# Projections to dt two at a time on two row quarters of the matmul array, with a re-laid opening and order, in a one-core decoder layer

## The chip, the cores and the metric

The kernel runs on one core of one Trainium2 chip. Times are microseconds on the device. The time before is the median of three runs: 1557.06 us (1556.51 to 1564.02). TensorE is called PE below, VectorE DVE, ScalarE ACT, GpSimd POOL, and the engine that only issues transfers SP.

## The reference, cut to what matters

A decoder layer of three post-norm blocks over 4 sequences of 512 tokens of width 512, all in float32: causal differential attention (8 head pairs of 128, four groups of keys and values), a Mamba-like selective scan over a second input `ctx`, and a mixture of 16 experts with a shared expert. The change sits in the second block:

```python
x = einsum('bld,ed->bel', ctx, in_proj_w)               # 256 -> 512 channels
x = silu(conv4_causal(x) + conv_b)
x_dbl = einsum('bdl,ed->bel', x, x_proj_w)              # 512 -> 16 + 16 + 16 rows
dt_low, Bm, Cm = split(x_dbl, [16, 32], axis=1)
dt = softplus(einsum('brl,dr->bdl', dt_low, dt_proj_w) + dt_proj_b)   # 16 -> 512 channels
state = state * exp(dt * A) + (dt * x) * Bm             # 512 steps, 16 states a channel
y = (sum(state * Cm) + D * x) * silu(z)
```

The contraction of the projection to dt is over 16 rows only.

## The kernel before, in words

The kernel does not call the engines directly. The class `Notes` records every instruction as a step with a key (about when it is wanted, plus a correction by result and engine from the table `SHIFT`), and the method `order` plays all steps against a list of costs and takes, for each engine, the ready step with the lowest key whose buffers are free. The result is a fixed order on each engine; on the chip each engine runs its own list strictly in order and waits for semaphores. So each engine's list depends on the keys, on `SHIFT` and on the buffers in each pool. Line 358 of the profile (`trace`) issues all of them, so lines in the profile are told apart by tile names, not by line numbers.

A float32 matmul in the source becomes two passes over the array, each with its own weight load; the profile counts passes. A projection to a 128 x 512 result over 512 rows is 4 matmuls, thus 8 passes.

The work falls in two stretches. For about two thirds of the time 16 units of attention (4 groups x 4 sequences) run on PE: projections `ps_qk` (q and k) and `ps_v`, scores `s`, transposes `pt`, values `po`, transposes `pt_o`, output projection `ps_out`. Beside them runs `scan(b)` for each sequence: `ps_in` (in-projection), copies to `xm`, four taps on ACT and DVE into `y`, silu (`sgc`), `ps_x` (48 rows), the copy `xd`, four matmuls `ps_dt` on 16 rows, softplus on ACT and DVE, and 32 scan steps on DVE. Then `experts(b)` runs: `pt_y`, `pt_x`, `ps_gate`, and for every expert `pg`, `ph`, `pa`; at the end `ps_y` and the last layer norm.

PSUM: `ps_in`, `ps_qk`, `ps_v`, `ps_x`, `ps_dt`, `ps_out` and others share the tag `mm` with three buffers, each free again when ACT or DVE has read it.

What stands around the opening: SP issues the first transfers in the listed order; PE starts with `ps_in` and goes on with `ps_qk`, `ps_x`, `ps_qk`, `ps_v`. DVE runs the taps, the silu products `y`, some small preparations (`lp`, `ls`, `nlam`, `a_neg`, which belong to the lambda of the attention and to A), and then adds the bias into `v`, which frees the PSUM of `ps_v`. POOL adds the output bias into the four residuals (`res<-res,obb`, 128 x 2048 each).

Of the kernel before, what the change touches and what calls it, by code (L numbers as in the profile page):

```python
# [20 lines left out]
ENGINES = ("tensor", "vector", "scalar", "gpsimd", "sync")  # L21

SHIFT = {
    "aT.s": 15.4, "a_neg.s": 12.1, "a_neg.v": -7.8, "bc.s": 7.4, "bq.s": -3.3, "bvb.s": -2.6, "cT.s": -3.5,
    "cf.v": -1.7, "cw.s": -2.2, "da.g": -4.8, "da.s": -1, "db.s": 4.2, "dsk.s": 2.1, "dt.s": -2.1, "dt.v": -7.7,
    "du.v": 21.2, "e.s": 7.6, "e.v": -2.1, "gb.s": -1.2, "h.v": -4.3, "ht.v": -6.5, "kT.s": 3.9, "l.v": 2.1,
    "ln_mv.v": -14.5, "ln_nb.v": -33.8, "ln_rs.g": -2.5, "ln_st.v": 4.7, "ln_ve.v": -21.4, "lo.v": 12.6, "lp.v":
    2.2, "ls.s": -1.8, "ls.v": -6.6, "lt.s": 3, "m.v": -3.7, "ms.v": -4.3, "nlam.v": -8.1, "o.s": -12.8, "oT.s":
    0.7, "obb.s": 17, "ow.s": -1.2, "pT.s": -2.7, "pa.t": 1, "pg.t": -2.1, "pg_s.t": -8.4, "ph.t": 2.8, "ph_s.t":
    3.2, "po.t": -7.2, "pr.s": -9.5, "pr.v": -13, "ps_dt.t": -0.1, "ps_gate.t": -18.9, "ps_in.t": -1.8,  # L30
    "ps_out.t": 5.1, "ps_qk.t": 1.3, "ps_v.t": 2.1, "ps_x.t": 12.8, "ps_y.t": 2.9, "pt.t": -0.3, "pt_o.t": 2.7,
    "pt_w.t": -7.1, "pt_x.t": 1.5, "pt_y.t": -5.9, "qT.s": 0.6, "relu.s": 20.5, "relu_s.s": -3.8, "res.g": -0.4,
    "res.s": -5.4, "res.v": -1.8, "rp.v": -16.4, "rs.g": 6.5, "rs.v": -12.2, "s.t": 0.9, "sc.v": 4, "sg.s": -1.5,
    "sg.v": 4.3, "sgc.s": 3.9, "sh.v": 7.5, "sp.v": 15.5, "sq.s": -16.2, "sub.s": -33.5, "sub.v": -9.9, "v.v":
    1.5, "w.s": 6.4, "wT.s": -1.1, "w_dg.s": 0.9, "w_dt.s": 6.5, "w_e.s": 23.5, "w_in.s": -30.8, "w_s.s": -0.3,
    "w_u.s": -4.7, "w_xp.s": 1.8, "wb.s": 10.2, "wq.s": 2.4, "wv.s": 5.9, "x2T.s": -13.1, "xd.s": 17.9, "xl.s":
    2.9, "xm.g": 1.7, "xm.s": 7.8, "xr.s": -1, "xw.v": 3.9, "y.g": -4.6, "y.s": 7.9, "y.v": -9.9, "yb.s": 5.6,
    "yb.v": 2.7,
}
B, S, HID = 4, 512, 512  # L40
NT = S // P
# [124 lines left out]
def cost(engine, name, out, ins, kw):  # L166

    n = columns(out) if isinstance(out, View) else 0
    psum = any(isinstance(v, View) and v.buf.pool.psum for v in ins)
    if engine == "tensor":  # L170
        if name == "transpose":
            return 0.11 * max(1, n / 128), 0.35, 0.0
        return max(n * 0.00168, 0.13), 0.35, 0.0
    if name == "dma_start":
        size = max(v.shape[0] * columns(v) * 4 if isinstance(v, View) else 0 for v in (out, *ins))
        add = kw.get("accum_op") is not None
        return {"sync": 0.45, "gpsimd": 0.95, "scalar": 0.1}[engine], 4.2 if add else 2.3, size / 230e3 * (1 + add)
    if engine == "gpsimd":
        if any(v is ALU.pow for v in ins):
            return 1.3, 0.5, 0.0  # L180
        return 0.15 + 0.0026 * n, 0.5, 0.0
    if engine == "scalar":
        wide = isinstance(kw.get("scale"), View) or isinstance(kw.get("bias"), View)
        return (
            0.19 + 0.00079 * n + (0.1 if wide else 0.0) + (0.15 if kw.get("accum_out") is not None else 0.0), 0.3, 0.0
        )
    if name == "tensor_tensor_scan":
        return 0.05 + 0.00223 * n, 0.25, 0.0
    if name in ("tensor_reduce", "bn_stats"):
        n = columns(ins[0])  # L190
    if n <= 8:
        return 0.2, 0.25, 0.0
    if name == "scalar_tensor_tensor":
        return 0.12 + 0.00125 * n, 0.25, 0.0
    if name == "tensor_scalar" and not psum:
        return 0.1 + (0.00085 if any(isinstance(v, View) for v in ins[1:]) else 0.00058) * n, 0.25, 0.0
    return 0.13 + (0.00108 if psum else 0.0011) * n + (0.1 if name == "tensor_tensor_reduce" else 0.0), 0.25, 0.0


class Notes:  # L200
# [7 lines left out]
    def note(self, engine, name, args, kw):  # L208
        s = Step()
        s.engine, s.name, s.args, s.kw, s.at = engine, name, args, kw, len(self.steps)  # L210
        out = kw["out"] if "out" in kw else args[0]
        rest = [a for a in args if a is not out] + [v for k, v in kw.items() if k not in ("out", "accum_out")]
        outs = [v for v in (out, kw.get("accum_out")) if isinstance(v, View)]
        ins = [v for v in rest if isinstance(v, View)]
# [38 lines left out]
    def order(self, keys, window=100.0):  # L253
# [24 lines left out]
        while events:  # L278
# [11 lines left out]
            for e in ENGINES:  # L290
# [4 lines left out]
                for s in ready[e]:  # L295
# [10 lines left out]

                    if all(
                        b in live
                        or free[b.pool, b.tag]
                        and (b.pool.psum or b in due[b.pool, b.counts[-1]][: free[b.pool, b.counts[-1]]])  # L310
                        for b in s.bufs
                    ):
                        best, least = s, rank
# [39 lines left out]
    def trace(self):  # L353
        done = self.order([s.key for s in self.steps])[0]
        assert len(done) == len(self.steps), "the order does not come to an end"
        for s in done:
            get = lambda v: v.get() if isinstance(v, View) else v
            getattr(getattr(self.nc, s.engine), s.name)(  # L358
                *[get(a) for a in s.args], **{k: get(v) for k, v in s.kw.items()}
            )  # L360
# [11 lines left out]
def decoder_kernel(  # L372
# [79 lines left out]
    def load_cT(b):  # L452
        return load([P, 2, S], ctxT[b].rearrange("(c p) t -> p c t", p=P), "h", "cT", 5)

    nc.key = -40.0
    bq = load([P, 32], bqkv, "bq")
    cw = load([P, ND, KC], convw, "cw")
    cb = load([P, ND], convb, "cb")
    w_in, cT0 = [], sb.tile([P, 2, S], "h", "cT", 5)
    for c in range(2):  # L460
        w_in.append(load([P, DI], inT[c * P : (c + 1) * P, :], "c2", "w_in", C2))
        nc.sync.dma_start(out=cT0[:, c, :], in_=ctxT[0, c * P : (c + 1) * P, :])
    xT0 = sb.tile([P, 4, S], "t8", "xT")
    wk0 = load_k(0)
    for c in range(4):
        nc.sync.dma_start(out=xT0[:, c, :], in_=xT[0, c * P : (c + 1) * P, :])
    wq0 = load_q(0)
    wv0 = load_v(0)
    w_xp = load([P, ND, 48], xpT.rearrange("(c p) n -> p c n", p=P), "w_xp")
    lt = load([P, 2, 2, HD], lam4.partition_broadcast(P).rearrange("p (a c d) -> p a c d", a=2, c=2), "qT", "lt", 2)  # L470
    sub = load([P, 2], subln, "sub")
    w_dt = load([DTR, DI], dtT, "c2", "w_dt", C2)
    db = load([P, ND], dtb, "db")
    dsk = load([P, ND], dskip, "dsk")
    a_neg = load([P, ND, NST], alog, "a_neg")
# [30 lines left out]
    def layernorm(src, dst, tiles=range(NT)):  # L506
# [12 lines left out]
        for i in tiles:  # L519
            nc.scalar.activation(  # L520
                dst[:, i, :], src[:, i, :], AF.Identity, bias=nb[:, i : i + 1], scale=rs[:, i : i + 1]
            )


    qk_scale = HD ** -0.5
# [121 lines left out]
    def scan(b):  # L647
# [23 lines left out]
            nc.vector.tensor_tensor(y[k], y[k], sg, ALU.mult)  # L671
        for d in range(ND):
            nc.tensor.matmul(
                px[:48, :], lhsT=w_xp[:, d, :], rhs=y[d // 2][:, d % 2, :], start=(d == 0), stop=(d == ND - 1)
            )
        xd = sb.tile([48, S], "c2", "xd", C2)
        nc.scalar.copy(xd, px[:48, :])
        nc.sync.dma_start(out=bc_d[b].rows(), in_=xd[DTR:48, :])


        nc.key = t_scan(b) - SOFTPLUS
# [1 line left out]
        for k in range(2):  # L683
            dt = sb.tile([P, 2, S], f"dt{k}", "dt")
            du = sb.tile([P, 2, S], f"du{k}", "du")
            lo = sb.tile([P, 2, S], "h", "lo", 5)
            for j in range(2):
                d = 2 * k + j
                pd = ps.tile([P, S], "mm", "ps_dt", 3)
                nc.tensor.matmul(pd, lhsT=w_dt[:, d * P : (d + 1) * P], rhs=xd[:DTR, :], start=True, stop=True)  # L690
                nc.scalar.activation(du[:, j, :], pd, AF.Abs, bias=db[:, d : d + 1])
                nc.scalar.activation(dt[:, j, :], pd, AF.Relu, bias=db[:, d : d + 1])
            nc.scalar.activation(du, du, AF.Exp, scale=-1.0)
# [51 lines left out]
    def experts(b):  # L745
# [26 lines left out]


        nc.key += 10.0
        pls, xr = [], sb.tile([P, NT, LAT], "pT", "xr", 2)
        for k in range(2):
            pl = ps.tile([P, 2, 256], "mm", "ps_gate", 3)
            for i in range(2):
# [165 lines left out]
```

## Time and profile before

| What | Before |
|---|---|
| Median of three runs | 1557.06 us (1556.51 to 1564.02) |
| The profiled execution: its own time, and its span from the first to the last instruction | 1558.77 us, 1557.0 us |
| PE busy with passes | 1534.4 us, 99% of the span, 4928 passes |
| DVE, ACT, POOL busy | 1204.0, 953.2, 193.9 us (77%, 61%, 12%) |
| Granted PE clock, mean | 0.992 |
| DMA moved | 196.18 MB, mean 126 GB/s |
| `ps_dt`: passes, busy | 32, 18.8 us |
| `ps_x`: passes, busy | 32, 16.9 us |

A busy row for PE counts each pass from its start to its modelled end. The ends overlap the next pass, so what a pass costs in a full stream is the distance between two starts, which is shorter than its listed duration. The clock column of a stretch is 1.00 when PE had its full clock and 0.50 when the throttle gave half.

### The profile page before, as it was taken

How to read it: one execution, taken by the hardware profiler on the slowest of the kernel's cores; microseconds unless marked ns; L12 is line 12 of the kernel's file. 1: busy time of each engine (PE TensorE's matmuls, PEld its weight loads, DVE VectorE, ACT ScalarE, POOL GpSimd, SP SyncE). 2: the span in 40 equal slices, each digit the busy share in tenths (PEclk: the TensorE clock that was granted, in tenths of full speed). 3: DMA queues.
4: the chain of work that ended last, by engine and by line, in shares of the span. 5: the costliest groups of instructions: out<-in, count | busy, mean ns of one | idle time of the engine just before them, and what ended most of it. 6: DMA issues, size and time to landing. Idle time of an engine off the chain costs nothing.

```text
span 1557.0 us, 15843 instructions
## 1 busy us (share of the span) xinstructions
PE 1534.4 (99%) x4928; PEld 846.0 (54%) x4928; DVE 1204.0 (77%) x2036; ACT 953.2 (61%) x2096; POOL 193.9 (12%) x208
## 2 busy tenths in 40 slices
PE   7999999999999999999999999999999999999998
PEld 2665665655656566565655555555545445445443
DVE  6559998777999887888988989999999962534433
ACT  3586566566756656576656658676967553444343
POOL 4011121101111111111111021211111100000000
PEclk9999999999999999999999999999999999999999
DMA  7126676525467763646765555665776851541341
GB/s 266 55 68 117 123 157 143 127 59 119 81 135 158 150 123 88 128 87 127 178 144 114 107 116 119 128 165 112 179 170 138 196 168 55 159 129 61 117 126 49
DMA packets 105523, 196.18 MB, mean 126 GB/s; under 512 B 10896, under 2 KB 45712, under 8 KB 105440
## 3 DMA queue, kind: packets, MB, share of 16 engines
q1 hardware_dynamic: 87008, 128.06, 29.1%
q0 software_dynamic: 18432, 67.12, 25.0%
q8 instruction: 39, 0.64, 0.2%
q14 instruction: 44, 0.36, 0.1%
HBM read 119.25 MB, written 75.89 MB: 125 GB/s over the span
## 4 chain that ended last, share of the span: by engine, by line
PE 96%; DVE 3%; ACT 0%; DMA 0%; issue 0%; SPq 0%; POOLq 0%; ACTq 0%
PE ps_qk L358 21%; PE ps_out L358 14%; PE s L358 9%; PE po L358 9%; PE ps_v L358 7%; PE pa L358 7%; PE ph L358 7%; PE pg L358 7%; PE ps_y L358 3%; PE pt L358 2%; PE pg_s L358 2%; PE ph_s L358 2%; PE pt_o L358 2%; PE ps_in L358 2%; PE ps_dt L358 1%; PE ps_gate L358 1%
## 5 line engine op out<-in xcount | busy, mean ns | idle before, releaser
L358 DVE TENSOR_TENSOR_SCAN h<-da,h 128x1024 f32<-128x1024 f32 x128 | 292.7, 2286 | 2.9 <-ACT da L358 0.4
L358 PE MATMUL ps_qk<-xT,wq 128*128 128x512 f32 x512 | 242.2, 594 | 0.0
L358 PE MATMUL ps_out<-ow,oT 128*128 128x512 f32 x512 | 238.1, 596 | 0.0
L358 POOL DMA_DIRECT2D y<-h x128 | 111.6, 872 | 795.1 <-DVE h L358 568.5
L358 ACT ACTIVATE da<-dt,a_neg 128x512 f32<-128x512 f32 (+1 forms) x256 | 175.1, 716 | 29.9 <-DVE h L358 25.9
L358 DVE TENSOR_TENSOR ht<-relu,ph 128x512 f32<-128x512 f32 x128 | 87.6, 685 | 125.3 <-PE ph L358 91.8
L358 ACT ACTIVATE relu<-pg 128x512 f32<-128x512 f32 x128 | 76.0, 593 | 160.4 <-PE pg L358 160.0
L358 PE MATMUL s<-kT,qT 128*128 128x384 f32 (+3 forms) x512 | 169.8, 440 | 1.1 <-DVE nm L358 1.1
L358 DVE CUSTOM_DVE_ANT_0 e<-s,mask 128x128 f32<-128x128 f32 (+3 forms) x256 | 118.9, 485 | 54.7 <-PE s L358 50.9
L358 PE MATMUL po<-v,pT 128*128 128x256 f32 x640 | 160.3, 381 | 0.4 <-ACT pT L358 0.4
L358 ACT ACTIVATE e<-e,nm 128x128 f32<-128x128 f32 (+3 forms) x256 | 142.0, 557 | 28.2 <-DVE nm L358 27.1
L358 DVE TENSOR_TENSOR h<-h,bc 128x1024 f32<-128x1024 f32 x128 | 156.2, 1220 | 1.3
L358 DVE TENSOR_TENSOR h<-du,bc 128x1024 f32<-128x1024 f32 x128 | 155.9, 1218 | 0.1
L358 PEld LDWEIGHTS po<-v,pT 128*128 128x128 f32 x640 | 121.7, 191 | 61.9 <-issue 35.2
L358 PEld LDWEIGHTS ps_out<-ow,oT 128*128 128x128 f32 x512 | 93.9, 192 | 83.7 <-issue 78.9
L358 PEld LDWEIGHTS ps_qk<-xT,wq 128*128 128x128 f32 x512 | 92.3, 191 | 77.3 <-issue 70.1
L358 PE MATMUL pa<-ht,w_e 128*128 128x512 f32 x256 | 130.8, 593 | 0.1
L358 PE MATMUL ph<-xw,w_e 128*128 128x512 f32 x256 | 130.3, 592 | 0.0
L358 PE MATMUL pg<-xl,w_e 128*128 128x512 f32 x256 | 129.4, 592 | 0.0
L358 PEld LDWEIGHTS s<-kT,qT 128*128 128x128 f32 x512 | 88.8, 192 | 63.5 <-issue 48.7
L358 PE MATMUL ps_qk<-xT,wk 128*128 128x512 f32 x256 | 120.9, 592 | 0.0
L358 ACT ACTIVATE sq<-po 128x256 f32<-128x256 f32 x128 | 48.7, 381 | 115.4 <-PE po L358 114.6
(121 smaller groups left out, 2084.0 us busy)
## 6 DMA issues: line engine op xcount, KB each, us to landing
y<-h POOLq DMA_DIRECT2D x128, 512.0 KB, 7.9
bc<-bc SPq DMA_DIRECT2D x64, 512.0 KB, 6.3
wb<-w SPq DMA_DIRECT2D x64, 256.0 KB, 3.4
xT<-in_xT_dram SPq DMA_DIRECT2D x15, 1024.0 KB, 7.8
w_e<-in_rwgT_dram SPq DMA_DIRECT2D x64, 128.0 KB, 2.2
w_e<-in_rw1T_dram SPq DMA_DIRECT2D x64, 128.0 KB, 2.3
w_e<-in_rw2T_dram SPq DMA_DIRECT2D x64, 128.0 KB, 2.5
wq<-in_wqkvT_dram SPq DMA_DIRECT2D x8, 512.0 KB, 5.9
```

Source lines behind the costliest of these rows:

```text
L358: getattr(getattr(self.nc, s.engine), s.name)(*[get(a) for a in s.args], **{k: get(v) for k, v in s.kw.items()})
```

## The change

1. The weights of the projection to x (`w_xp`) grow from 48 to 96 columns: the 16 dt columns and 16 that follow them go to columns 0 to 31, the same again to 32 to 63, and B and C to 64 to 95, so that `xd` holds the dt rows twice, at partitions 0 and 32. The weights `w_dt` are loaded twice, to partitions 0 and 32.
2. Two matmuls of `ps_dt` are noted as one step `pair`: it takes two `mm` buffers at once and issues the two matmuls one right behind the other, the first on rows 0 to 15, the second on rows 32 to 47.
3. The opening: eight matmuls of the identity on itself (`warm`) stand first on PE; the transfers of the first `ctx` halves (`cT`) are issued by ACT instead of SP; `bq` is loaded later, `w_in` first.
4. The tile `xr` of the experts moves from the pool tag `pT` to `c2`.
5. `SHIFT` has new values throughout, so the order on all engines is a new one.

```diff
-    "aT.s": 15.4, "a_neg.s": 12.1, "a_neg.v": -7.8, "bc.s": 7.4, "bq.s": -3.3, "bvb.s": -2.6, "cT.s": -3.5,
...
+    "aT.s": -4.1, "a_neg.s": 14.4, "a_neg.v": -15.4, "bc.s": 5.7, "bq.s": -18.3, "bvb.s": 8.1, "cT.s": -3.2,
...
     if engine == "tensor":
+        if name == "pair":
+            return 0.15 + n * 0.00168, 0.35, 0.0
...
-                        or free[b.pool, b.tag]
+                        or free[b.pool, b.tag] >= (2 if s.name == "pair" and b.pool.psum else 1)
...
+            if s.name == "pair":
+                for k in range(0, len(s.args), 3):
+                    out, lhsT, rhs = (get(v) for v in s.args[k : k + 3])
+                    self.nc.tensor.matmul(out, lhsT=lhsT, rhs=rhs, start=True, stop=True)
+                continue
...
-    nc.key = -40.0
-    bq = load([P, 32], bqkv, "bq")
-    cw = load([P, ND, KC], convw, "cw")
-    cb = load([P, ND], convb, "cb")
+    nc.key = -60.0
     w_in, cT0 = [], sb.tile([P, 2, S], "h", "cT", 5)
     for c in range(2):
         w_in.append(load([P, DI], inT[c * P : (c + 1) * P, :], "c2", "w_in", C2))
-        nc.sync.dma_start(out=cT0[:, c, :], in_=ctxT[0, c * P : (c + 1) * P, :])
+        nc.scalar.dma_start(out=cT0[:, c, :], in_=ctxT[0, c * P : (c + 1) * P, :])
+    nc.key = -50.0
+    cw = load([P, ND, KC], convw, "cw")
+    cb = load([P, ND], convb, "cb")
+    nc.key = -40.0
...
+    bq = load([P, 32], bqkv, "bq")
...
-    w_xp = load([P, ND, 48], xpT.rearrange("(c p) n -> p c n", p=P), "w_xp")
+    w_xp = sb.tile([P, ND, 96], "w_xp")
+    for to, src in ((0, 0), (32, 0), (64, DTR)):
+        nc.sync.dma_start(
+            out=w_xp[:, :, to : to + 32], in_=xpT[:, src : src + 32].rearrange("(c p) n -> p c n", p=P)
+        )
...
-    w_dt = load([DTR, DI], dtT, "c2", "w_dt", C2)
+    w_dt = sb.tile([48, DI], "c2", "w_dt", C2)
+    for row in (0, 32):
+        nc.sync.dma_start(out=w_dt[row : row + DTR, :], in_=dtT)
...
+    nc.key = -60.0
+    pw = ps.tile([P, S], "tr", "warm", 1)
+    for i in range(8):
+        nc.tensor.matmul(pw[:, :P], lhsT=ident, rhs=ident, start=True, stop=True)
...
-                px[:48, :], lhsT=w_xp[:, d, :], rhs=y[d // 2][:, d % 2, :], start=(d == 0), stop=(d == ND - 1)
+                px[:96, :], lhsT=w_xp[:, d, :], rhs=y[d // 2][:, d % 2, :], start=(d == 0), stop=(d == ND - 1)
...
-        xd = sb.tile([48, S], "c2", "xd", C2)
-        nc.scalar.copy(xd, px[:48, :])
-        nc.sync.dma_start(out=bc_d[b].rows(), in_=xd[DTR:48, :])
+        xd = sb.tile([96, S], "c2", "xd", C2)
+        nc.scalar.copy(xd, px[:96, :])
+        nc.sync.dma_start(out=bc_d[b].rows(), in_=xd[64:, :])
...
-            for j in range(2):
+            pds, both = [ps.tile([P, S], "mm", "ps_dt", 3) for _ in range(2)], []
+            for j, pd in enumerate(pds):
+                d, row = 2 * k + j, slice(32 * j, 32 * j + DTR)
+                both += [pd, w_dt[row, d * P : (d + 1) * P], xd[row, :]]
+            nc.tensor.pair(*both)
+            for j, pd in enumerate(pds):
                 d = 2 * k + j
-                pd = ps.tile([P, S], "mm", "ps_dt", 3)
-                nc.tensor.matmul(pd, lhsT=w_dt[:, d * P : (d + 1) * P], rhs=xd[:DTR, :], start=True, stop=True)
...
-        pls, xr = [], sb.tile([P, NT, LAT], "pT", "xr", 2)
+        pls, xr = [], sb.tile([P, NT, LAT], "c2", "xr", C2, 1)
```

In the new order of PE's list the four matmuls of `ps_x` of the first sequence stand after `ps_v` and the first scores, where before they stood among the first `ps_qk`. Before, the 16 matmuls of `ps_dt` stood in 13 groups; now there are 8 pairs, no two next to each other. DVE's list begins with all twelve taps, then both products `y`, `lp`, `ls`, `a_neg`, `nlam`, and then `v`. On SP the fourth residual stands behind the second `xT`, which waits for the first one to be read.

More of the change, by code (lines that the diff above doesn't have):

```diff
@@ L23 @@
 SHIFT = {
-    "aT.s": 15.4, "a_neg.s": 12.1, "a_neg.v": -7.8, "bc.s": 7.4, "bq.s": -3.3, "bvb.s": -2.6, "cT.s": -3.5,
[L25 to L38, printed above, removed]
+    "aT.s": -4.1, "a_neg.s": 14.4, "a_neg.v": -15.4, "bc.s": 5.7, "bq.s": -18.3, "bvb.s": 8.1, "cT.s": -3.2,
@@ new lines @@
+    "cb.s": 8.1, "cf.v": -3.1, "cw.s": -23.6, "da.g": -2.3, "da.s": -4.8, "db.s": 14.1, "dsk.s": -4.9, "dt.s":
+    -1.3, "dt.v": 15.1, "du.s": 0.1, "du.v": 29.2, "e.s": 10.8, "e.v": -2.3, "gb.s": -19.3, "h.v": -4.8, "ht.v":
+    -0.1, "kT.s": 14.9, "l.v": 4.2, "ln_mv.v": -1.1, "ln_nb.v": -31.4, "ln_rs.g": -13.8, "ln_st.v": 3.6,
+    "ln_ve.v": 3.4, "lo.v": 13.6, "lp.v": 42.6, "ls.s": -0.8, "ls.v": -22.4, "lt.s": 18.3, "m.v": 14, "ms.v":
+    -4.2, "nlam.v": -10.2, "o.s": -36.7, "oT.s": -2.6, "obb.s": 11.9, "ow.s": 12.6, "pT.s": 0.4, "pa.t": -10.2,
@@ new lines @@
+    "pg.t": -2.1, "pg_s.t": -9.5, "ph.t": 2.9, "ph_s.t": 6.7, "po.t": -5.2, "pr.s": -30, "pr.v": -30.1, "ps_dt.t":
+    -16.9, "ps_gate.t": -16.7, "ps_in.t": -4.3, "ps_out.t": 5.2, "ps_qk.t": -0.8, "ps_v.t": 3.2, "ps_x.t": -10,
+    "ps_y.t": 24.2, "pt.t": 0.1, "pt_l.t": -22.6, "pt_o.t": 3.8, "pt_w.t": -18.3, "pt_x.t": 0.2, "pt_y.t": -7.6,
+    "qT.s": -3.4, "relu.s": 2.7, "relu_s.s": -17.2, "res.g": -21.2, "res.s": 8.5, "res.v": -8.5, "rp.v": 13.1,
+    "rs.g": -1.6, "rs.v": -1.6, "s.t": 0.9, "sc.v": 7.9, "sg.s": -0.4, "sg.v": 2.4, "sgc.s": 2.2, "sh.v": -3,
@@ L39 @@
+    "sp.v": 22.6, "sq.s": 6.5, "sub.s": -30.9, "sub.v": -23.8, "v.v": -2.7, "w.s": -13.4, "wT.s": 1.8, "w_dg.s":
+    -8.9, "w_dt.s": 37.8, "w_e.s": 29.7, "w_in.s": -30.3, "w_s.s": -8.9, "w_u.s": 29.3, "w_xp.s": 13.9, "warm.t":
+    -7.8, "wb.s": 19.6, "wk.s": -11.5, "wq.s": 2.5, "wv.s": 8.9, "x2T.s": 9.1, "xT.s": -1.8, "xd.s": 26, "xl.s":
+    4.6, "xm.g": 22.4, "xm.s": 6, "xr.s": -5.8, "xw.v": 6.8, "y.g": -12.6, "y.s": 9.9, "y.v": -40.6, "yb.s": -5.9,
+    "yb.v": -6.4,
 }
@@ L213, in note @@
         outs = [v for v in (out, kw.get("accum_out")) if isinstance(v, View)]
+        if name == "pair":
+            outs, rest = list(args[0::3]), [*args[1::3], *args[2::3]]
         ins = [v for v in rest if isinstance(v, View)]
```

## The prediction

> **What bounds the kernel now.** I read the page first (shares, clock, chain), then PE's groups, then PE's waits, then stretches with the clock, then the timeline where the clock or PE stood.
>
> ```profile
> PE 1534.4 (99%) x4928; PEld 846.0 (54%) x4928; DVE 1204.0 (77%) x2036; ACT 953.2 (61%) x2096; POOL 193.9 (12%) x208
> ...
> PE 96%; DVE 3%; ACT 0%; DMA 0%; issue 0%; SPq 0%; POOLq 0%; ACTq 0%
> ...
> L358 PE MATMUL ps_dt<-xd,w_dt 16*128 16x512 f32 x32 | 18.8, 683 | 0.0
> ...
> PE ps_in L358 <- DMA cT<-in_ctxT_dram: 5.9, 1, 5.9
> PE ps_x L358 <- DVE y L358: 5.3, 1, 5.3
> ```
>
> PE is the bound from end to end; DVE's 3% of the chain is the opening. So a microsecond off PE's stream is a microsecond off the time, and a new gap in it is one on it. What a pass costs is read between starts, not from durations:
>
> ```profile
> 14.79 5.31 PE L358 MATMUL ps_qk<-xT,wk 128*128 128x512 f32 x12
> ...
> 95.22 0.61 PE L358 MATMUL s<-kT,qT 128*128 128x128 f32 x4
> 95.75 1.98 PE L358 MATMUL ps_dt<-xd,w_dt 16*128 16x512 f32 x4
> 97.66 0.70 PE L358 MATMUL s<-kT,qT 128*128 128x256 f32 x2
> 98.20 0.60 PE L358 MATMUL pt<-ident,e 128*128 128x128 f32 x4
> ```
>
> Twelve 512-column passes take 5.31 us, the last 0.59: (5.31-0.59)/11 = 0.429 us a pass; in the same way 0.215 for 256 columns, 0.109 for 128. Summed over all passes this is 1511.5 us. PE's first pass starts at 5.86, its last at 1549.5; only about 32 us of that stretch is not plain passes. A `ps_dt` pass on 16 rows costs the same 0.429, and going in and out costs more: dt starts 0.09 late after four 0.109 passes, the next `s` stands at 97.66 where four passes from 95.75 end at 97.47 (0.19), and `pt` comes 0.10 late: 0.39 us a group.
>
> The clock is the third thing. Stretches, first for `ps_dt` alone (PE, weight load and ACT busy, clock, DMA), then for all engines after two of them:
>
> ```profile
> 95.20:98.62 3.42, 1.98 (x4) 0.66 (x4) 1.71 (x3) 1.00 0.97 151
> 371.68:375.10 3.42, 2.22 (x5) 0.48 (x3) 2.37 (x4) 1.00 1.08 289
> 654.99:658.40 3.41, 2.71 (x7) 0.81 (x6) 2.46 (x5) 1.00 1.00 131
> 931.47:934.88 3.41, 2.02 (x5) 0.42 (x4) 2.62 (x4) 1.00 0.00 0
> ...
> 375.10:378.51 3.41, 3.41 (x6) 1.17 (x5) 1.84 (x3) 1.44 (x4) 0.61 (x1) 0.50 0.44 138
> 378.51:381.93 3.42, 3.42 (x7) 2.03 (x7) 1.71 (x4) 1.34 (x3) 0.24 (x1) 0.50 0.48 104
> ```
>
> After the two stretches with 2.2 us or more of dt the clock falls to 0.50 for two stretches (6.83 us, also 658.4 to 665.2); after those with 2.0 us it does not. PE never stood idle there. Each fall costs 6.83/2 = 3.4 us.
>
> **The change, part by part** (minus is gained).
>
> *dt pairs.* 16 matmuls are 32 passes. The two matmuls of a pair are issued one behind the other: A1 A2 B1 B2. No row shows two row quarters at work together. Bounds: nothing overlaps (4 slots, 0) to both matmuls side by side (2 slots, 8 x 0.86 = -6.9). [...] I take 8 x 0.429 = **-3.4**. Groups: 13 become 8 (the order's list): 5 x 0.39 = **-2.0**. A pair and its entry is 1.3 + 0.2 us, and no two pairs stand within 6 us, so no stretch reaches 2.2 us of dt: both clock falls go, **-6.8**. [...]
>
> *96 columns.* Pass length is by the 512 moving columns; weight loads of 128 columns (0.19) hide under 0.429. The 48-column groups of the later sequences cost 1.25 us in such edges; 96 columns may be treated as the full array. Bounds -1.25 to 0.2; I take **-1.2**. The copy `xd` (0.58) is by columns: nothing.
>
> *Opening, start.* `ident` is written at 1.7 us; 16 warm passes at half clock are 16 x 0.218 = 3.5, so `ps_in` starts at about 5.2. `cT` goes out on ACT's queue from about 0.75 (two issues, at SP's 0.45 each; ACT then stood idle 8.7 us before its first copy, which hides them and the table load) and with 3.7 us to landing is there at 4.9. **-0.65**. From 5.86 to 9.87 the passes ran at half clock (2.1 us lost); warmed, I allow 0.35: **-1.75**.
>
> *Opening, `ps_x`.* Before, PE waited 5.3 us at `ps_x` and then ran at half clock to 37.2; with edges 8.15 us. `ps_x` now stands behind `ps_v`, so this goes. But see who was late:
>
> ```profile
> 22.26 19.07 POOL L358 TENSOR_TENSOR res<-res,obb 128x2048 f32<-128x2048 f32 x4 [7.49 <-DMA obb<-in_ob_dram]
> ...
> 22.30 4.76 DVE L358 TENSOR_TENSOR lp<-lt 128x256 f32<-128x256 f32 x1
> 27.43 5.07 DVE L358 TENSOR_TENSOR y<-y,sgc 128x1024 f32<-128x1024 f32 x1
> 32.42 4.45 DVE L358 TENSOR_TENSOR nlam<-ls 128x1 f32<-128x1 f32 x1
> 36.98 4.40 DVE L358 TENSOR_SCALAR a_neg<-a_neg 128x64 f32<-128x64 f32 x1
> 42.10 0.42 DVE L358 TENSOR_TENSOR v<-ps_v,bvb 128x256 f32<-128x256 f32 x1 [0.72 <-PE ps_v L358]
> ```
>
> While POOL adds, each of these DVE instructions, however small, lasts until one add of 4.7 us ends. In the new list `lp`, `a_neg`, `nlam` stand ahead of `v`, three adds are in a row, and nothing shows that they start much later than 22 (the bytes asked for ahead of them are the same, 5.7 MB). My count: taps end at 20.2, the products at 22.7, so `lp`, `a_neg`, `nlam` pay 3 x 4.7 to 36.6, and the first `v` is out at 37. PE needs it for the fourth `ps_v`: 5.2 + 0.3 + 16 x 0.43 + 32 x 0.43 + 24 x 0.215 = 31.3. It stands 5.7 us and then loses some 2.5 to the clock, as before: **0**. If the adds start a microsecond after `lp`, one fewer is paid: -5.6; one later still, -8.15.
>
> *Queues.* SP loses two `cT` issues, gains two of `w_xp` and one of `w_dt` (0.45 each), the last behind residuals and `ow`; they are wanted at 45 us, about 20 us later. The fourth residual waits on SP behind `xT` until `xT0` is read (46 us), so its add falls on DVE's softmax around 55; the transposes stand 7 us behind their scores with 3 to 4 needed, so a 4.5 us block leaves **+1** (0 to 4). Behind that add on POOL stands `rs`, wanted only after the head's last `po`, near 67. `xr` in `c2`: between `ps_gate` and its transposes the new list has 2.1 us of passes or more, before 2.2: nothing.
>
> *New order.* Work on DVE and ACT is the same; I compared how many microseconds of passes lie between a result and its reader. Before, the near ones (0 to 0.6) are where the trace has waits: 1042 to 1053 (about 4 us), 1257 (0.9), the end (0.8). The new list has the same ones and two more (a score behind DVE's `e`, a `po` behind `pT`); the first pair stands 1.4 us behind `ps_x` with the 0.58 copy `xd` between: **+1** (-2 to +5).
>
> Sum: -3.4 -2.0 -6.8 -1.2 -0.65 -1.75 +0 +1 +1 = -13.8. The profiled execution's own 1558.77 becomes 1545; that execution lies 1.7 us above the median of the runs, so against 1557.06 it is **1543**.
>
> **The rivals.** (A) The above, collision moved from `ps_x` to `v`: 0.46, own range 1538 to 1548. (B) The adds start later than `lp`: one or two blocks are spared: 1543 - 5.6 = 1537; for it, obb's load waits in SP's queue for a `wq` to land; 0.30. (C) The pair does not do what it says: quarters run one after another. Then -3.4 goes and a pair with edges is 2.0 us of dt, at the edge of the clock's fall; one or two falls of 3.4: 1543 + 3.4 + 5 = 1551; 0.16, about half of it inside 0.5%. (D) Slower: a pair needs two of three `mm` buffers at once and ACT holds them for four reads (4 x 0.69, in strict order behind softmax work; before, the first read came 5 us after the pass). The remaining groups then wait for one buffer. At 3 us a pair, 8 x 3 = 24: 1567; it decides from 2.7 us a pair. Against it: in the new list the next taker of a pair's buffer stands 3.8 us or more behind it, before 2.2; and the three-buffer waits cost nothing before. 0.08.
>
> **How the numbers follow.** 0.5% (7.8 us, about what a measurement of this kernel tells from no change) is 1549.3 and 1564.8. Faster: A, B and half of C, 0.46 + 0.30 + 0.07 = 0.83; same: the rest of C, 0.09; slower: D, 0.08. The range 1531 (B with a two-slot pair and no new waits) to 1552 (C) leaves D and the tails out.
>
> **What would show it.** Right: clock 1.00 around all dt pairs; about 1.3 us from a pair's first pass to the next matmul; PE's longest wait no longer at `ps_x` but at `ps_v` <- DVE `v`, with POOL adding beside it; first `ps_in` near 5.2. Wrong: any half-clock stretch after dt; 1.7 us a pair; waits of `ps_qk` or `ps_out` on ACT `du`; `lp`, `a_neg`, `nlam` short.

## The result: faster, and the profile after

The changed kernel takes 1535.99 us (median of six runs, 1533.76 to 1542.19) where the kernel before takes 1556.99 (six runs beside it, 1555.96 to 1564.29): a ratio of 0.986, 95% interval 0.983 to 0.989. A second occasion (f1, below) gave 1536.2 against 1558.73, 0.985 (0.982 to 0.988). The profiled execution took 1535.82 us, its span is 1534.0; before it was 1558.77 and 1557.0. So 22.95 us went between the two profiled executions (21.0 between the medians), where the sum had 13.8.

From the page of the changed kernel, the busy times and the chain:

```profile
PE 1518.6 (99%) x4944; PEld 847.1 (55%) x4944; DVE 1197.0 (78%) x2036; ACT 950.0 (62%) x2092; POOL 195.5 (13%) x208
...
PE 97%; DVE 2%; ACT 1%; issue 0%; POOL 0%; POOLq 0%; ACTq 0%; DVEq 0%
```

PE is still the bound from end to end. It carries 16 passes more (the warm ones) and is busy 15.8 us less. From its groups, kept apart by shape (passes, busy, mean ns):

```profile
L368 PE MATMUL ps_x<-y,w_xp 128*96 128x512 f32 x32 | 14.6, 592 | 0.0
...
L366 PE MATMUL ps_dt<-xd,w_dt 16*128 16x512 f32 x32 | 9.0, 640 | 0.0
```

`ps_dt` had 18.8 and `ps_x` 16.9. The 32 passes of `ps_dt` are the same number and none is shorter (the shortest is listed with 587 ns in both kernels); two run in the time of one. PE's waits after:

```profile
PE po L368 <- ACT pT L368: 2.0, 2, 1.6
PE pt_y L368 <- DVE res L368: 1.8, 2, 1.0
PE warm L368 <- POOL ident masks.py:199: 1.8, 1, 1.8
PE ps_v L368 <- DVE v L368: 1.2, 1, 1.2
```

The 5.3 us at `ps_x` is gone. The wait that the prediction put in its place, at `ps_v` for DVE's `v`, is there, but with 1.2 us and not 5.7. The first pair in PE's timeline (start, duration of the group):

```profile
46.39 3.60 PE L368 MATMUL ps_x<-y,w_xp 128*96 128x512 f32 x8
...
49.94 1.47 PE L368 MATMUL s<-kT,qT 128*128 128x512 f32 x6
51.33 1.13 PE L366 MATMUL ps_dt<-xd,w_dt 16*128 16x512 f32 x4
52.39 1.13 PE L368 MATMUL po<-v,pT 128*128 128x256 f32 x4
```

From the pair to the next pass is 1.06 us; before, four `ps_dt` passes took 1.91. The trace's own starts of the four passes are 51.333, 51.340, 51.866 and 51.873: two start 7 ns apart, the other two half a microsecond later, again 7 ns apart. Passes of one matmul, on the same rows, stand 0.429 us or more apart in the row of before (and in e1 below), so it is one pass of each matmul that runs beside one of the other. The pair takes two slots, plus 0.38 us for going in and out, of which 0.20 lies inside the 1.06. Whether PE brought the passes into this order or got them so, the trace does not show. `ps_x` with 96 columns has no such edges: eight passes of 0.43 from 46.39 end at 49.83, where the next pass starts.

The clock, by stretches, first of two with a pair in them (for `ps_dt` alone), then around the one fall of the whole run after the opening (all engines):

```profile
348.93:352.35 3.42, 1.13 (x4) 0.30 (x4) 1.27 (x2) 1.00 0.63 126
...
905.31:908.72 3.41, 1.13 (x4) 0.30 (x4) 1.07 (x3) 1.00 0.46 40
```

```profile
1017.95:1021.36 3.41, 1.45 (x10) 0.79 (x8) 2.83 (x6) 1.32 (x4) 0.00 (x0) 1.00 0.81 169
1021.36:1024.77 3.41, 3.23 (x9) 2.34 (x10) 3.34 (x10) 2.10 (x8) 1.01 (x1) 0.50 0.97 259
```

No pair is followed by a fall. The one at 1021 is new: three short waits (0.78 and 1.00 us for DVE's `res`, then 0.36 for ACT's `pT`, which reaches into the next stretch) came close together, PE was busy for 1.45 of 3.41 us, almost all of it with transposes (`pt_y`, `pt`), and the next stretch ran at 0.50. It cost 1.7 us.

The opening, in DVE's timeline and POOL's:

```profile
21.44 2.36 DVE L368 TENSOR_TENSOR y<-y,sgc 128x1024 f32<-128x1024 f32 x2
23.71 0.42 DVE L368 TENSOR_TENSOR lp<-lt 128x256 f32<-128x256 f32 x1
24.17 0.42 DVE L368 TENSOR_REDUCE ls<-lp 128x2 f32<-128x256 f32 x1
24.66 3.90 DVE L368 TENSOR_SCALAR a_neg<-a_neg 128x64 f32<-128x64 f32 x1
28.48 4.51 DVE L368 TENSOR_TENSOR nlam<-ls 128x1 f32<-128x1 f32 x1
...
33.11 1.09 DVE L368 TENSOR_TENSOR v<-ps_v,bvb 128x256 f32<-128x256 f32 x3
```

```profile
23.96 9.01 POOL L368 TENSOR_TENSOR res<-res,obb 128x2048 f32<-128x2048 f32 x2 [21.66 <-DMA res<-in_x_dram]
34.04 4.52 POOL L368 TENSOR_TENSOR res<-res,obb 128x2048 f32<-128x2048 f32 x1 [1.06 <-DMA res<-in_x_dram]
```

The first add began at 23.96, a quarter of a microsecond after `lp` had begun. `lp` was out in 0.42; only `a_neg` and `nlam` each lasted to the end of an add, and the three `v` that had piled up came at 33.1, not at 37. The reduction `ls` between them took 0.42 us in the middle of the first add, so the add did not hold every instruction of DVE that works in SBUF. This is the prediction's case B, with the adds after `lp`. That was chance, as f1 shows.

### The profile page after: what moved, and what is told of

It reads as the page before. It is cut to its first block, busy times and chain, and to the rows that moved or that the text cites. A ratio compares the mean times of both kernels' runs of the same rounds, so it can differ in the third digit from the quotient of the medians.

```text
span 1534.0 us, 15805 instructions
## 1 busy us (share of the span) xinstructions
PE 1518.6 (99%) x4944; PEld 847.1 (55%) x4944; DVE 1197.0 (78%) x2036; ACT 950.0 (62%) x2092; POOL 195.5 (13%) x208
## 4 chain that ended last, share of the span: by engine, by line
PE 97%; DVE 2%; ACT 1%; issue 0%; POOL 0%; POOLq 0%; ACTq 0%; DVEq 0%
PE ps_qk L368 20%; PE ps_out L368 14%; PE s L368 9%; PE po L368 9%; PE pa L368 7%; PE ph L368 7%; PE pg L368 7%; PE ps_v L368 7%; PE ps_y L368 3%; PE pt L368 2%; PE pt_o L368 2%; PE pg_s L368 2%; PE ph_s L368 2%; PE ps_in L368 2%; PE ps_gate L368 1%; PE ps_x L368 1%
## 5 line engine op out<-in xcount | busy, mean ns | idle before, releaser
L368 PE MATMUL ps_qk<-xT,wq 128*128 128x512 f32 x512 | 237.3, 593 | 0.0
L368 PE MATMUL s<-kT,qT 128*128 128x384 f32 (+3 forms) x512 | 165.4, 435 | 0.0
L368 PE MATMUL ps_v<-wv,xT 128*128 128x256 f32 x512 | 118.5, 379 | 1.2 <-DVE v L368 1.2
```

What stands on the lines that cost most here:

```text
L368: getattr(getattr(self.nc, s.engine), s.name)(*[get(a) for a in s.args], **{k: get(v) for k, v in s.kw.items()})
```

## The experiments

Theory 1 (mine after the result): the two row quarters run side by side, which is worth 6.8 us; the clock falls follow stretches with much 16-row work in them; and how many of DVE's small instructions fall under a POOL add decides some 5 us of the opening. The rivals: the pairs gain by their grouping alone, the falls are due to something else, and the opening's gain comes from the new transfers or from the warm passes.

**e1_same_rows**: the changed kernel with both matmuls of a pair on the same 16 rows; every engine's order is the same.

```diff
-                d, row = 2 * k + j, slice(32 * j, 32 * j + DTR)
+                d, row = 2 * k + j, slice(0, DTR)
```

> The changed kernel, with both matmuls of a pair on rows 0 to 15; every engine's order stays. Theory 1 (the two row quarters really work together, two slots instead of four; and the clock falls after a stretch of 3.41 us with some 2.0 to 2.2 us of dt in it): four slots a pair, 8 x 0.86 = 6.9 us more, and each pair now has 1.72 + 0.3 = 2.0 us of dt at the edge, so 0 to 3 falls of 3.4 us: span 1541 to 1551 against 1534. Rival 1 (clock falls have nothing to do with the rows in use): 1541 and the clock 1.00 at all pairs. Rival 2 (a pair gains nothing over two matmuls one after another): 1534.

Measured: 1540.68 us (four runs, 1539.01 to 1542.05), ratio 0.9875 (0.9853 to 0.9896), span 1540.0. PE's timeline at the pair that starts at 349.01 in the changed kernel, and two stretches with a group of four passes in them, with the stretch behind each:

```profile
349.97 1.98 PE L366 MATMUL ps_dt<-xd,w_dt 16*128 16x512 f32 x4
351.88 0.70 PE L368 MATMUL s<-kT,qT 128*128 128x256 f32 x2
```

```profile
348.93:352.35 3.42, 1.98 (x4) 0.66 (x4) 1.05 (x2) 1.00 0.88 183
352.35:355.76 3.41, 0.00 (x0) 0.00 (x0) 0.61 (x2) 1.00 0.04 8
635.65:639.07 3.42, 1.98 (x4) 0.66 (x4) 1.47 (x3) 1.00 0.04 7
639.07:642.48 3.41, 0.00 (x0) 0.00 (x0) 0.95 (x2) 1.00 0.00 0
```

A pair now takes 1.91 us from its start to the next pass instead of 1.06: 8 x 0.85 = 6.8 us. That is the worth of the second row quarter by itself. The spans differ by 6.0, because this run's opening was 0.7 us shorter by other means (one cold pass fewer, no waits at 57). And the 1.98 us of 16-row passes in each of these two stretches brought no fall.

**e2_before_96_rows**: the kernel before, with the rows and columns of the projections filled up with zeros to 96.

```diff
-    w_xp = load([P, ND, 48], xpT.rearrange("(c p) n -> p c n", p=P), "w_xp")
+    w_xp = sb.tile([P, ND, 96], "w_xp")
+    nc.gpsimd.memset(w_xp[:, :, 48:], 0.0)
...
+    w_dt = sb.tile([96, DI], "c2", "w_dt", C2)
+    nc.gpsimd.memset(w_dt, 0.0)
...
-                nc.tensor.matmul(pd, lhsT=w_dt[:, d * P : (d + 1) * P], rhs=xd[:DTR, :], start=True, stop=True)
+                nc.tensor.matmul(pd, lhsT=w_dt[:, d * P : (d + 1) * P], rhs=xd, start=True, stop=True)
```

> The kernel before, with each dt matmul over 96 rows: weights filled up with zeros to 96 rows, w_xp and xd with zeros to 96; still 32 dt passes in 13 groups, no pairs, the old opening. Theory 1 (few active rows let the clock fall; changing to and from few rows or columns costs the edges): both falls near 375 and 658 us go (-6.8), the edges of dt (-5.1) and of ps_x (-1.5) go: span 1543.6 against 1557.0, clock 1.00 there, the opening with its wait and its own fall as before. Rival 1 (the falls come from something else in these stretches, such as transposes, and would stay): 1550, clock 0.50 in two stretches.

Measured: 1547.24 us (seven runs, 1540.03 to 1552.16), ratio 0.9926 (0.9902 to 0.995), span 1550.4. Stretches of this kernel, for `ps_dt` alone, each with the one behind it:

```profile
373.88:377.29 3.41, 2.55 (x6) 1.06 (x6) 1.27 (x2) 1.00 0.77 205
377.29:380.70 3.41, 1.38 (x3) 0.30 (x2) 2.54 (x4) 1.00 0.89 239
653.78:657.19 3.41, 3.29 (x8) 0.88 (x6) 2.79 (x5) 1.00 0.92 121
657.19:660.61 3.42, 0.10 (x1) 0.00 (x0) 2.17 (x4) 1.00 0.57 102
```

Up to 3.29 us of `ps_dt` in a stretch, and the clock stays at 1.00: in the kernel before, 2.22 us of 16-row passes brought it down. So between these two kernels the falls went with the rows in use, not with the tile, the place or the weight loads (1.06 and 0.88 us of them in the fuller stretches here, 0.48 and 0.81 before). The edges are gone too: four passes on 96 rows start at 100.41 and the next pass at 102.13, 1.72 us for 4 x 0.43. In the profiled execution, the longest of the seven, 13.3 us of falls and edges went and some 6.7 came back: most of it in the opening, where PE's wait at `ps_x` for DVE's `y` was 9.7 us instead of 5.3, with one of the taps under an add as well, ahead of `lp` and `y`, and 0.9 in a new wait of `ps_qk` for ACT's `du`. So its span is that of the rival, but the clock rows are not. Without pairs and without a second copy of the dt rows this kernel gains 11 of the change's 21 us in the median.

**e3_old_shift**: the changed kernel with the table `SHIFT` of the kernel before, and so close to that kernel's order.

```diff
-    "aT.s": -4.1, "a_neg.s": 14.4, "a_neg.v": -15.4, "bc.s": 5.7, "bq.s": -18.3, "bvb.s": 8.1, "cT.s": -3.2,
...
+    "aT.s": 15.4, "a_neg.s": 12.1, "a_neg.v": -7.8, "bc.s": 7.4, "bq.s": -3.3, "bvb.s": -2.6, "cT.s": -3.5,
...
```

> The changed kernel with the old table SHIFT, so another order; pairs, doubled weights, warm passes and the transfers of cT on ACT as in the change. Theory 1 (the gain is made by pairs, clock and the moved ps_x; the order elsewhere is worth little): span 1532 to 1541; in the opening DVE has y, nlam and a_neg behind lp again, so a wait of PE at ps_v of 1 to 6 us. Rival 3 (the new order carries the gain): 1548 or more.

Measured: 1541.45 us (four runs, 1540.98 to 1541.91), ratio 0.9883 (0.9866 to 0.99), span 1539.4. Its wait, and a stretch behind it:

```profile
PE ps_v L367 <- DVE v L367: 5.5, 1, 5.5
```

```profile
34.07:37.48 3.41, 0.00 (x0) 0.00 (x0) 3.41 (x3) 0.00 (x0) 3.41 (x2) 0.50 0.01 2
```

Here the second product `y`, `nlam` and `a_neg` each fall under an add (4.04, 4.46 and 4.38 us in DVE's timeline), three in all as in the prediction's case A; PE stands 5.5 us and the clock falls for two stretches. The wait is 4.3 us longer than in the changed kernel and the last eight `ps_v` at half clock cost 1.7 more; with half a microsecond less elsewhere that is the 5.4 us of span between the two. The new order brings nothing else that can be seen.

**e4_pairs_alone**: the kernel before with parts 1 and 2 of the change alone, the pairs with their 96 columns and doubled weights; the old `SHIFT`, transfers and no warm passes.

```diff
...
+            pds, both = [ps.tile([P, S], "mm", "ps_dt", 3) for _ in range(2)], []
+            for j, pd in enumerate(pds):
+                d, row = 2 * k + j, slice(32 * j, 32 * j + DTR)
+                both += [pd, w_dt[row, d * P : (d + 1) * P], xd[row, :]]
+            nc.tensor.pair(*both)
...
```

> The kernel before with the pairs alone (96 columns, weights twice, two mm buffers a pair); old SHIFT, old opening without warm passes. Theory 1: pairs -6.9, edges of dt -2.0, edges of ps_x -1.3, two clock falls -6.8: span 1540 against 1557 if the opening loses as before (PE waits some 5 us for DVE under POOL's adds); up to 6 less if the order moves ps_x behind ps_v there. Rival 3 (the opening and the order carry the gain): 1550 or more.

Measured: 1544.35 us (four runs, 1542.69 to 1546.87), ratio 0.9903 (0.9882 to 0.9924), span 1541.0. PE's first two waits:

```profile
PE ps_in L367 <- DMA cT<-in_ctxT_dram: 6.8, 1, 6.8
PE ps_v L367 <- DVE v L367: 3.5, 1, 3.5
```

`ps_dt` is busy 9.0 us and `ps_x` 14.7, as in the full change, and no pair is followed by a fall. Two thirds of the gain (14 of 21 us) come with the pairs and their 96 columns, among them that the planner puts `ps_x` behind `ps_v` here too, so that the wait of 5.3 became one of 3.5. The other third is the opening: `ps_in` starts at 6.81 and loses 2.9 us to the cold clock, where the changed kernel starts at 5.33 and loses 1.1.

**e5_no_pool_adds**: the changed kernel without the four bias adds on POOL.

```diff
+            if s.engine == "gpsimd" and s.name == "tensor_tensor" and s.args[0].buf.name.startswith("res"):
+                continue
```

> The changed kernel without POOL's four adds of the output bias into the residuals (that part is left out); every other instruction and order stays. Theory 4 (PE's 1.2 us wait at ps_v, and the waits near 57 and 60 us, come from DVE instructions that last until a POOL add ends): a_neg and nlam take under 0.5 us each, no wait of PE at ps_v, none at 57 to 61: span 1531.8 against 1534.0. Rival 4 (DVE is late there for its own work or for transfers): a_neg and nlam or the waits stay, 1534.

Measured: 1532.74 us (one run), span 1530.7. DVE's timeline at the two instructions that took 3.90 and 4.51 us:

```profile
23.46 0.20 DVE L370 TENSOR_SCALAR a_neg<-a_neg 128x64 f32<-128x64 f32 x1
...
24.13 0.16 DVE L370 TENSOR_TENSOR nlam<-ls 128x1 f32<-128x1 f32 x1 [0.47 <-ACT ls L370]
```

Without the adds they take 0.20 and 0.16, PE has no wait at `ps_v` and none at 57. That is some 2.2 us of the 3.3 in span; 1.1 is the clock, which was up before `ps_in` began in this run: its 16 passes took 6.87 us to the first `ps_qk`, 0.429 each.

**e6_pool_busy_early**: the changed kernel with two POOL products (128 x 1022, from `sgc` into the still unused `da`) put ahead of the adds, so that POOL is busy when `lp` comes.

```diff
...
+                for _ in range(2):
+                    self.nc.gpsimd.tensor_tensor(to[:, :, 1:].get(), g[:, :, 1:].get(), g[:, :, 1:].get(), ALU.mult)
...
```

> The changed kernel with two more POOL products of 128 x 1022, from the first sgc into a scratch tile, ahead of the four adds, so that POOL is busy from about 21.5 instead of 24 us. Theory 4: the products y, lp, a_neg and nlam each last until one POOL instruction ends (2.3 us for the new ones, 4.6 for the adds), v comes some 5 to 8 us later, PE waits 6 to 9 us at ps_v and the clock falls after it (1.7 to 3.4): span 1541 to 1545. Rival 4: DVE shares the time and v is late by the 4.6 us of added work at the most in part; wait at ps_v under 3 us, no fall of the clock, under 1537.

Measured: 1542.0 us (one run), span 1538.9. DVE's timeline:

```profile
25.58 2.11 DVE L375 TENSOR_TENSOR lp<-lt 128x256 f32<-128x256 f32 x1
...
28.06 4.06 DVE L375 TENSOR_SCALAR a_neg<-a_neg 128x64 f32<-128x64 f32 x1
32.04 4.50 DVE L375 TENSOR_TENSOR nlam<-ls 128x1 f32<-128x1 f32 x1
```

PE's wait at `ps_v` grows from 1.2 to 4.6 us and the clock falls from 35.24 to 42.06; 4.9 us of span. That is less than the theory's wait of 6 to 9 us and its span of 1541 or more, but with the fall that the rival had excluded. Nothing on DVE or PE was changed: POOL alone, which is busy 13% of the time and has 0% of the chain, moves the end.

**e7_v_first**: the changed kernel with `a_neg` and `nlam` behind the third `v` in DVE's list.

```diff
+        late = [s for s in done if s.engine == "vector" and s.args and isinstance(s.args[0], View) and s.args[0].buf.name in ("a_neg", "nlam")]
+        done = [s for s in done if s not in late]
...
+        done = done[: third + 1] + late + done[third + 1 :]
```

> The changed kernel with a_neg and nlam moved behind the third v on DVE; all else in its order. Theory 4: v is free of POOL's adds, PE's wait at ps_v (1.3 us with its edge) goes and nothing takes its place, since nlam then falls between two adds: span 1532.6 against 1534.0, and a narrower spread of times. Rival 4: 1534, the wait stays at ps_v; or nlam meets the third add and the scores wait instead, 1534 to 1537.

Measured: 1533.54 us (four runs, 1533.41 to 1534.32), ratio 0.9842 (0.9809 to 0.9874), span 1531.6. The adds and the first `v`:

```profile
23.81 13.75 POOL L372 TENSOR_TENSOR res<-res,obb 128x2048 f32<-128x2048 f32 x3 [21.50 <-DMA res<-in_x_dram]
...
29.07 0.43 DVE L372 TENSOR_TENSOR v<-ps_v,bvb 128x256 f32<-128x256 f32 x1 [4.40 <-PE ps_v L372]
```

The adds run to 37.56, and each `v` comes right behind its `ps_v` in the middle of them, in 0.42 us: the adds did not hold `v`, which reads PSUM. `a_neg` and `nlam` take 0.25 and 0.15 behind it, at the seam between the second and the third add. PE has no wait at `ps_v`. Of the 2.4 us of span, some 0.9 is that this execution has no clock fall near 1021, so about 1.5 belong to the move.

**e8_pt_y_three**: the changed kernel with the transposes `pt_y` in the three `mm` buffers instead of their own one; it was to remove the waits at 1018 to 1021, and it puts more takers on the buffers that the pairs need.

```diff
-            pt = ps.tile([P, S], "tr", "pt_y", 1)
+            pt = ps.tile([P, S], "mm", "pt_y", 3)
```

> The changed kernel with the transposes pt_y in the mm buffers (three) instead of the single tr buffer; the order around the start of each experts() changes with it. Theory 5 (the waits near 1018 to 1024 and at 1237 are transposes that wait for DVE to empty their only buffer, with a fall of the clock behind the first): waits of pt_y on DVE res go (1.8 us), with the wait of pt behind it (1.0) and the fall (1.7): span 1529 to 1531. Rival 5 (mm buffers become scarce for ps_out and ps_qk, or the layer norm behind pt_y sets the time): 1533 to 1538.

Measured: 1561.18 us (twelve runs, 1555.3 to 1564.65), ratio 1.0013 (0.9994 to 1.0033), span 1553.5. The waits of `pt_y` for `res` went, and these came, with the clock of a long stretch:

```profile
PE pt_o L368 <- ACT o L368: 5.8, 1, 5.8
PE pt L368 <- DVE e L368: 4.7, 1, 4.7
```

```profile
1083.31:1103.79 20.48, 9.70 (x23) 5.86 (x24) 19.31 (x17) 13.89 (x25) 5.95 (x6) 0.50 0.90 155
```

The buffer is an input to the planner, so the order around the first `experts` changed with it, and PE ran into DVE and ACT there: busy for 9.7 of 20.5 us, at half clock, so that 20.5 - 9.7/2 = 15.6 of the 19.5 us of span that it takes more are lost in this one stretch. Theory and rival had at most 1538, so both failed. The run says little on the buffer itself.

**f1_after_again, f2_v_first_again, f3_no_warm**: the changed kernel, e7's kernel, and the changed kernel without the warm passes, side by side.

> The changed kernel as it is, run side by side with the two below, to see what of its spread belongs to the opening. Theory: its time moves with how many of DVE's small instructions fall under a POOL add of 4.5 us; in the profile shown two did, at a price of 2.2 us on PE, and a third would cost some 4 to 6 more. Expect a median of 1535 to 1537 and a range of at least 5 us (1533 to 1541). Rival: the spread is the chip's alone and has nothing to do with the opening; then this kernel and the one with v ahead spread alike.

> The same kernel with a_neg and nlam behind the third v in DVE's list, against f1 on the same chip. Theory: with no DVE instruction left under the first three adds that PE waits for, the time is 1533 to 1534.5 in nearly every run, range under 2 us, 2 to 3 us below f1's median. Rival: equal medians and equal spread, the earlier difference of 2.4 us being one between occasions.

> The changed kernel without the 16 warm passes. The prediction gave the warm passes and the early load together -2.4 us; measured -1.5. Theory: PE then waits for cT alone and starts ps_in at 4.5 to 5.3, but at half clock until about 9.5 (8.3 to 11.7): 1.7 to 2.7 us lost to the cold clock instead of 1.1, less up to 0.8 from the earlier start: ps_qk starts at 13.0 to 14.8 instead of 13.3, the time 0 to +1.5 against f1. Rival: the warm passes bring the clock up by their 3.4 us whole; then ps_qk starts 2 us or more later and the time rises by as much.

Measured: f1 1536.2 us (six runs, 1534.19 to 1541.29), f2 1533.83 (six, 1532.83 to 1539.37), f3 1541.06 (six, 1535.65 to 1542.86). The profiled execution of f1, the changed kernel to the letter, was its longest, 1541.29 us. Its POOL adds began at 22.51, where the first profile had 23.96. POOL's timeline, DVE's, and PE's wait:

```profile
22.51 14.32 POOL L368 TENSOR_TENSOR res<-res,obb 128x2048 f32<-128x2048 f32 x3 [20.20 <-DMA res<-in_x_dram]
```

```profile
23.27 4.73 DVE L368 TENSOR_TENSOR lp<-lt 128x256 f32<-128x256 f32 x1
...
28.38 4.05 DVE L368 TENSOR_SCALAR a_neg<-a_neg 128x64 f32<-128x64 f32 x1
32.35 4.50 DVE L368 TENSOR_TENSOR nlam<-ls 128x1 f32<-128x1 f32 x1
...
36.96 1.08 DVE L368 TENSOR_TENSOR v<-ps_v,bvb 128x256 f32<-128x256 f32 x3
```

```profile
PE ps_v L368 <- DVE v L368: 5.5, 1, 5.5
```

This is the prediction's case A, instruction by instruction: `lp`, `a_neg` and `nlam` pay for three adds, `v` comes at 37.0, PE stands 5.5 us. One kernel has both cases, and the start of the first add against `lp` picks one. Of twelve runs of this kernel nine lie at 1533.8 to 1536.6 and three at 1540.7 to 1542.2; one of each group was profiled, so that the other ten divide by the same cause is likely, not shown.

f2's median is 2.4 us below f1's, as in the first comparison; the ranges overlap in single runs. My expectation of a narrow range failed: in f2's profiled execution, its longest, PE waited elsewhere.

```profile
PE ps_v L372 <- ACT qT L372: 3.4, 1, 3.4
```

```profile
33.19 0.20 ACT L372 ACTIVATE ls<-ls 128x2 f32<-128x2 f32 x1 [8.04 <-DVE ls L372]
33.30 0.67 ACT L372 ACTIVATE qT<-ps_qk,bq 128x512 f32<-128x512 f32 x1
```

With the adds at 22.39, a product `y` and `lp` each paid; ACT's `ls` waits for DVE's `ls` behind `lp`, `qT` stands behind it on ACT and frees PE's buffer late. So there is a second path from POOL to PE, over ACT, that the prediction didn't have.

f3: `ps_in` starts at 4.60 instead of 5.33 but runs at half clock for longer (9.26 us to the first `ps_qk` against 7.56 in f1), and `ps_qk` starts at 13.86 where f1 has 12.89 and f2 13.27. The warm passes are worth 0.5 to 1.0 us there, within the theory's bounds. The 4.9 us of its median are more than the theory's 1.5 and more than the later `ps_qk`, which was the rival's ground; in its profiled execution a `y` (and `lp` and `a_neg`) fell under the adds and PE waited at `ps_v` 3.4 us for ACT's `qT` and 1.8 for DVE's `v`, so in that execution most of it is the collision. Whether the later `lp` meets the adds in most runs was not measured.

**f4_lambda_last**: e7's kernel with `lp` and both `ls` behind the third `v` as well.

```diff
-        late = [s for s in done if s.engine == "vector" and s.args and isinstance(s.args[0], View) and s.args[0].buf.name in ("a_neg", "nlam")]
+        late = [s for s in done if s.engine in ("vector", "scalar") and s.args and isinstance(s.args[0], View) and (s.args[0].buf.name in ("lp", "ls", "nlam") or (s.engine == "vector" and s.args[0].buf.name == "a_neg"))]
```

> As f2, with lp and both ls (DVE's sum and ACT's exponential) moved behind the third v as well, so that neither v on DVE nor qT on ACT stands behind an instruction that a POOL add can hold. In f2's profile the adds began at 22.4, ahead of lp; lp took 4.72, ACT's ls waited 8.0 for it, qT stood behind ls, and PE 3.4 at ps_v. Theory: that second path goes too, whenever the adds begin; no wait of PE at ps_v above 0.3, median 1532 to 1534, range under 2 us where f2 had 1532.8 to 1539.4. Rival: what the adds hold is paid further on (the softmax e behind lp, pt behind it), and single runs of 1537 and more remain.

Measured: 1535.19 us (four runs, 1534.71 to 1535.39), ratio 0.9853 (0.9834 to 0.9872), span 1533.3. The adds began early (22.67), `lp` paid 4.61 us, and PE had no wait at `ps_v`, only 0.6 at a score behind DVE's maximum. So the second path is cut and the range is 0.7 us; but the median missed the 1532 to 1534 expected. Its span is 1.7 above e7's: 0.7 in the opening, and 1.0 at the waits and the clock fall near 1020, a fall that e7's profile doesn't have. Between the changed kernel and these two versions no more than 2.4 us is at stake, and which of the two is better is open; e7's has the lowest median.

## Why the prediction was right in kind and 7 us too high

The time came within its range, at the number of rival B and not at the central one. Term by term, in us of the profiled executions (start-to-start distances against the 0.429, 0.3225, 0.2155 and 0.109 of plain passes):

| Term | Predicted | Measured | From |
|---|---|---|---|
| Pairs side by side | -3.4 | -6.8 | 1.06 a pair; e1: 1.91 |
| Edges of dt groups | -2.0 | -2.0 | 13 x 0.39 to 8 x 0.38 |
| Clock falls at dt | -6.8 | -6.8 | two to none |
| 96 columns | -1.2 | -1.25 | `ps_x` without edges |
| `ps_in` earlier | -0.65 | -0.5 | 5.86 to 5.33 |
| Cold clock | -1.75 | -0.9 | 2.07 to 1.13 lost |
| `ps_x` wait turned `ps_v` wait | 0 | -6.7 | 8.15 to 1.45 |
| Fourth add | +1 | +0.8 | short waits from 57 to 61 |
| New order | +1 | +1.6 | fall at 1021, `po` at 1064, older waits gone |
| End | 0 | -0.3 | |

**The pair term was half its size.** The 8 x 0.429 took one slot off each pair, a choice between the bounds of none and two, and so expected three slots and 1.3 us a pair. No run shows a pair of three slots. The trace has a pass of one matmul and a pass of the other starting 7 ns apart, and the same again 0.53 us later: two slots, 1.06 us from the pair to the next pass, against 1.91 on the same rows (e1). The bound of -6.9 was the one that came, with -6.8. The prediction wrote the passes in the order of the source, A1 A2 B1 B2; they started as one of each, twice.

**The collision was case B in the profiled execution.** The step was "nothing shows that they start much later than 22". The first add began at 23.96 there and at 22.51 in f1; `lp` began at 23.71 and 23.27. That 1.4 us of difference between two executions of one kernel is worth 5.5 us, and the prediction had both cases with their prices: -5.6 for one block fewer. With two slots a pair the sum would be 1545 - 3.4 - 5.6 = 1536.0 for the first profile, which took 1535.82, and 1545 - 3.4 = 1541.6 for f1, which took 1541.29. That the sums come so close is in part luck: other terms missed by up to a microsecond and cancel. So what failed was the choice of case, not the mechanism. And it was not one that the profile could settle: I should have given the cases as two outcomes of one kernel. The ground given for B, a late load of `obb`, is also not what made the adds late: `obb` was asked for at 15.18 and took 4.8 us to land, and the trace has POOL wait for the first residual `res` (its line above), which SP issued behind `obb`, at 16.22 in the first profile and at 15.27 in f1.

**The clock falls were right.** Before, the clock fell with PE never idle, after 2.22 and 2.71 us of 16-row passes in a stretch; with 16-row passes down to 1.06 us a stretch, or with the same passes on 96 rows (e2, up to 3.29 us), no stretch with dt is followed by a fall. e1 leaves it at 1.98 us, no fall, as the rows of before had it with 1.98 and 2.02. With full matmuls alone beside the idle time, the clock fell after 2.05 us idle in f1 (30.61 to 34.02, PE busy for 1.36) and did not after 1.93 in f3 (29.73 to 33.14, busy for 1.48). That a 16-row pass weighs as little as an idle PE, and that about 2 us of such time in 3.41 is where the falls begin, is an estimate of mine from these rows; what decides a fall was not shown.

One limit on idle time would not cover all the rows, though. In e5 the clock fell after the first of these stretches and stayed up after the second, in which PE was busy for less:

```profile
1015.51:1018.93 3.42, 1.86 (x11) 1.34 (x12) 3.28 (x11) 0.50 (x3) 0.32 (x1) 1.00 0.96 184
1059.89:1063.30 3.41, 1.78 (x9) 1.31 (x8) 3.34 (x9) 3.40 (x9) 0.41 (x1) 1.00 0.51 132
```

Of the 1.86 us, 1.33 are transposes (`pt_y`, `pt`, `pt_o`), of the 1.78 only 0.27, and the stretch ahead of the fall at 1021 had 1.96 us idle and transposes in nearly all the rest. That transposes, too, weigh less than other passes would fit these three stretches; it was not shown, as no run varied them alone.

**The rest.** Cold clock: the clock came up at 7.60 us, 2.3 us into `ps_in`, and I had allowed a loss of 0.35 us; in other runs of the same passes up to 1.3 us were lost (e6). The buffers (D) never bound: in the changed kernel PE has no wait at `ps_qk` or `ps_out` for ACT's `du`, and with the pairs in the old order (e3, e4) one of 0.5 us. The chance that the pair does nothing (C) is ruled out by e1. The new order cost what was allowed, in part by a fall that nobody had counted: three waits of up to a microsecond from 1018 on come together among transposes. The move of `xr` was not tried alone; none of PE's waits names it.

## What to carry to other kernels

The small matmuls on 16 rows cost three times here: a full pass each (0.429 us), an edge at every change of the rows in use (0.39 us a group), and the clock where they bunched (two falls of 3.4 us, after 2.22 and 2.71 us of them in a stretch). Packing two on separate row quarters halved the first (1.06 us a pair against 1.91), thinned out the second (13 groups to 8) and ended the third; filling the rows with zeros to 96 ended the last two alone (e2). Before trusting a forecast for an opening, look for an engine off the path (here POOL, at 13%) that can hold small instructions of another one (here `nlam`, 4.51 us instead of 0.16): list what stands behind each of them, on every engine, and treat a start that is uncertain by a microsecond as two outcomes. Put the instructions that can be held behind those that the bounding engine waits for.

## What the runs showed of the hardware that I had not expected

- Two 16-row matmuls on row quarters 0 and 1, issued one behind the other, each of two passes, ran pass beside pass: starts 7 ns apart, 1.06 us for all four against 1.91 on the same rows (e1).
- Going in and out of 16-row passes cost 0.38 to 0.39 us a group; of 96-row passes (e2: four in 1.72 us) and 96-column passes (eight in 3.44 us), nothing that can be seen. 48 columns had cost 1.25 us in all.
- The clock fell after a stretch with 2.22 us of 16-row passes in it (before); it did not after 3.29 us of 96-row passes (e2) or after 1.98 of 16-row ones (e1). In e5 it fell with PE busy for 1.86 of 3.42 us, mostly with transposes, and did not with PE busy for 1.78 of 3.41, mostly with other passes.
- A POOL add of 128 x 2048 held a DVE instruction on one column (`nlam`) for 4.51 us, to 32.99, where the second add ends at 32.97; without the adds it took 0.16 (e5), and at the seam between two adds 0.15 (e7). The adds did not hold `v`, which reads PSUM (0.42 us in the middle of them, e7), nor the reduction `ls` (0.42 us under the first add).
- The start of POOL's first add differed between two executions of one program by 1.4 us (22.51 in f1 and 23.96), and these two differed by 5.5 us in time.
